# Window attention and a depthwise convolution on one core: where the last taps and the last turn of the fifteenth image stand on VectorE

## The chip, the cores and the metric

The kernel runs on one core of a Trainium2 chip. The time is device time in microseconds (us), from runs of the whole program. PE is the matrix engine, DVE the vector engine, ACT the scalar engine, POOL the GpSimd engine; SP issues DMAs. A trace is one profiled execution.

## The reference

The input x has 16 images of 56 x 56 positions with 384 channels. Two layers follow each other:

```python
x = x + window_attention(group_norm(x))   # 7 x 7 windows, shifted by 3, 12 heads of 32, mask, relative bias
x = x + depthwise_conv(group_norm(x))     # 3 x 3, one filter per channel, weights reduced to their signs
```

Each group norm has 32 groups of 12 channels and takes mean and variance over a whole image. So the second layer of an image can begin only when the first layer of that image is complete.

## The kernel before, in words

Channels lie on the partitions, in three blocks of 128 (c = 0, 1, 2). An image is 8 strips of 7 rows (s counts strips over all images), a strip is 2 units of 4 windows. There are 256 units (u). The loop in `all_units` does, for unit u, the sums of the exponentials (`add_up`, L646, PE), their inverse (`invert`, L685 to L688, ACT and DVE), the products with the values (`attend`, L667), the division (`divide`, L695, DVE), for each second unit the projection (`project`, L706 on PE, L714 and L720 on DVE, a copy L726 on POOL and the store of the strip to a DRAM tile `mid`, L730 and L732), and for unit u + 1 the scores (L576, PE), the softmax's scaling and bias (`softmax`, L593, DVE) and its exponential (`exponential`, L611, ACT).

The second layer of image b - 1 runs beside the first layer of image b. It works in six chunks: half an image (k = 0, 1) of one channel block. For a chunk, `band` loads rows of `mid`, `pad` writes the normalized rows into a padded tile (`hps`, two of them, L798), `middle` writes the centre tap and the residual into a sum (`accs`, two of them, L826 or L828), eight calls of `tap` (L834, DVE) add the other taps into it, `turn_sum` transposes it by blocks of 32 x 32 in place (L841, DVE), and eight calls of `store` (L848, on SP's queue) write it out.

The order of these pieces is written by hand. `at(when, f, ...)` puts a call on a list under a time in units; `all_units` issues the heavy work of unit u in six steps, and after each step the listed calls whose time has come. Each engine executes its instructions in the order of issue. A DMA on SP stands in SP's queue, and what is issued later on SP comes behind it.

The last image (b = 15) has no next image to hide behind. `plan_last` orders its second layer: from unit 254.8 on, `band_late` loads, part 0, the rows that already are in `mid` (L779: into spare tiles, among them `qk` and `bias`), and, part 1, the rows of the last strip. `late_norm` calls `norm_products`, which finds the group means by products with a matrix on PE (L362: `pm` for the means, `pv` for the variances) instead of a trip through DRAM, with short DVE operations in between (L351 to L387). `center` follows (L741 to L745), and then the chunks of channel blocks 0 and 1 with taps on DVE, and channel block 2 as `convolve` on PE (L871, L878), four pieces of 14 rows, whose sums `carry` copies with ACT (L886) and stores. The last two chunks on DVE are turned by PE (L904, L906, L912).

`norm_products` has an argument `meanwhile`: calls to be issued while PE forms the products. The first stands between the products of the means and L375, the rest between the products of the variances and L383. At the start of the program it is used for two weight operations.

The chunk that the change touches is the last one of image 14 (k = 1, c = 2). Its padded tile is the second of `hps`, its sum the second of `accs`. `plan_conv` puts its taps 0 to 8 and its turn at equal distances in units 252 to 254, and its stores, 0.1 units apart, where `plan_last` has the loads of `band_late`, also 0.1 units apart. The sum tile is written again by the second chunk of the last image (L828, o<-qk, on ACT).

Of the kernel before, what the change touches and what calls it, by code (L numbers as in the profile page):

```python
# [22 lines left out]
def group_blocks(nch, gsize, P=128):  # L23

    n = nch // P
    return [
        (k, m)
        for m in range(n)
        for k in range(n)
        if (k * P) // gsize <= ((m + 1) * P - 1) // gsize and (m * P) // gsize <= ((k + 1) * P - 1) // gsize  # L30
    ]
# [3 lines left out]
def kernel(  # L35
# [14 lines left out]
    B, H, W, C = x.shape  # L50
    NH = rel_table.shape[1]
    D = C // NH
    NC = C // P
    HPC = P // D
# [9 lines left out]
    NB = H // BR  # L64
# [28 lines left out]
    def bank(name):  # L93
        return ps.tile([P, 512], F32, tag="mm", name=name)
# [221 lines left out]
    late_tiles = {}  # L316
# [29 lines left out]
    def norm_products(key, gm, meanwhile=()):  # L346
        st = stats.pop(key)
        name = "%d_%d" % key
        mv = small.tile([P, NC, 2], F32, tag="mv", name=f"mv{name}")
        for c in range(NC):  # L350
            nc.vector.bn_aggr(mv[:, c, :], st[:, c].rearrange("p s k -> p (s k)"))  # L351
        if key[0]:
            nc.vector.tensor_tensor(mv[:, :, 0], mv[:, :, 0], bo_sb, ALU.add)

        def group_mean(x, name):
            pg = bank(name)
            pairs = group_blocks(C, GS)
            for m in range(NC):
                of_m = [n for n, (k, j) in enumerate(pairs) if j == m]
                for n in of_m:  # L360
                    k = pairs[n][0]
                    nc.tensor.matmul(  # L362
                        pg[:, 4 * m : 4 * m + 1],
                        gm[:, n, :],
                        x[:, k : k + 1],
                        start=(n == of_m[0]),
                        stop=(n == of_m[-1]),
                    )
            return pg[:, : 4 * NC].rearrange("p (m f) -> p m f", f=4)[:, :, 0]

        mean = group_mean(mv[:, :, 0], f"pm{name}")
        for f, n in meanwhile[:1]:
            f(n)
        dev = small.tile([P, 3, NC], F32, tag="dev_late", name=f"dev{name}", bufs=1)
        nc.vector.tensor_copy(dev[:, 2], mean)  # L375
        nc.vector.tensor_tensor(dev[:, 0], mv[:, :, 0], dev[:, 2], ALU.subtract)
        nc.vector.tensor_tensor(dev[:, 0], dev[:, 0], dev[:, 0], ALU.mult)
        nc.vector.tensor_tensor(dev[:, 0], dev[:, 0], mv[:, :, 1], ALU.add)
        var = seen[:, B : B + NC] if key[0] else dev[:, 0]
        spread = group_mean(dev[:, 0], f"pv{name}")  # L380
        for f, n in meanwhile[1:]:
            f(n)
        nc.vector.tensor_scalar(var, spread, EPS, None, ALU.add)  # L383
        nc.gpsimd.tensor_tensor(dev[:, 1], var, power.to_broadcast([P, NC]), ALU.pow)
        coef = small.tile([P, NC, 2], F32, tag="coef", name=f"coef{name}", bufs=4)
        nc.vector.tensor_copy(coef[:, :, 0], dev[:, 1])
        nc.vector.scalar_tensor_tensor(coef[:, :, 1], dev[:, 2], -1.0, dev[:, 1], ALU.mult, ALU.mult)  # L387
        coefs[key] = coef
# [1 line left out]

    def late_norm(b):
        norm_products((1, b), late_tiles["gm"])

    xs = {}

# [516 lines left out]
    def plan_last(b, first):  # L914

        chunks = [(k, c) for k in range(NB) for c in range(NC - 1)]
        bands_late = [(0, NC - 1), chunks[0], (1, NC - 1), chunks[1], (2, NC - 1), chunks[2], (3, NC - 1)]
        for n, (k, c) in enumerate(bands_late):
            at(first - 1.2 + 0.1 * n, band_late, b, k, c, 0)
            at(first - 0.04 + 0.001 * n, band_late, b, k, c, 1)  # L920
        at(first, late_norm, b)
        at(first + 0.1, center, b, nc.vector)
        for n, (k, c) in enumerate(chunks):
            when = first + 1 + n
            if n == len(chunks) - 1:
                for part in range(2):
                    at(when - 1.9, band_late, b, k, c, part)
            at(when - 0.6 if n else when - 0.13, pad, b, k, c)
            at(when - 0.5 if n else when - 0.12, middle, b, k, c, False, n == 0)
            for i, t in enumerate((0, 1, 2, 3, 5, 6, 7, 8)):  # L930
                at(when + i / 8, tap, b, k, c, t)
            if k == 0:
                at(when + 0.99, turn_sum, b, k, c)
                for part in range(2 * HPC):
                    at(when + 1.01 + 0.05 * part, store, b, k, c, part)
            else:
                for half in range(2):
                    at(when + 1.3 + 0.01 * half, turn_late, b, k, c, half, n == len(chunks) - 1)
            k, c = n, NC - 1
            at(when - 0.3 if n else when - 0.11, pad, b, k, c, True)  # L940
            at(when - 0.25 if n else when - 0.1, middle, b, k, c, True, n == 0)
            at(when + 0.1, convolve, b, k, c, 0)
            at(when + 0.4, convolve, b, k, c, 1)
            at(when + 1.1, carry, b, k, c)
# [4 lines left out]
    def at(when, f, *args):  # L949
        side.setdefault(int(when), []).append((when, f, args))  # L950

    def plan_conv(p, first, step, lead, late, queue):

        at(first, norm_gather, (1, p), queue)
        at(first + 0.1, norm_scale, (1, p), queue)
        at(first + 0.2, center, p)
        first += lead
        for n in range(NB * NC):
            k, c = divmod(n, NC)
            when = first + step * n  # L960
            at(max(when - 1.22 * step, first - lead + 0.5), band, p, k, c)
            at(when - 0.35 * step, pad, p, k, c)
            at(when - 0.25 * step, middle, p, k, c)
            for i, t in enumerate((0, 1, 2, 3, 5, 6, 7, 8)):
                at(when + step * i / 9, tap, p, k, c, t)
            at(when + step * 8 / 9, turn_sum, p, k, c)
            for part in range(2 * HPC):
                at(when + step * 8 / 9 + late + 0.1 * part, store, p, k, c, part)
# [42 lines left out]
    def plan(last_queue):  # L1011
        for b in range(1, B):
            plan_load(b)
            plan_conv(b - 1, NU * b, 2.6 if b < B - 1 else 1.95, 3, 0.4, nc.gpsimd)
        at(B * NU - 6, fetch_late)
        for t in range(9):
            at(B * NU - 5 + 0.3 * t, diagonal, t)
        plan_last(B - 1, B * NU)
# [51 lines left out]
    with tc.manual_schedule():  # L1070
# [7 lines left out]
        gm = bpool.tile([P, BR + 2, R], F32, tag="xb", name="gm_first").rearrange("p h w -> p (h w)")  # L1078
        pairs = len(group_blocks(C, GS))
        gm = gm[:, : pairs * P].rearrange("p (n q) -> p n q", q=P)  # L1080
# [6 lines left out]
        for s in range(NS):  # L1087
            for c in range(NC):
                load(s, c)
        fetch_weights(NC, xpool.tile([P, NC, ST], F32, tag="x", name="wl_out"))  # L1090
        norm_products((0, 0), gm, ((turn_weights, 2), (load_weights, 2)))
        load_bias(nc.sync, 0, 16, True)
        load_bias(nc.gpsimd, T - 1, T, True)
# [94 lines left out]
```

## Time and profile before

| | |
|---|---|
| median of 3 runs | 4023.74 us (4023.71 to 4024.25) |
| the profiled execution | 4024.73 us |
| its span, first to last instruction | 4022.9 us |
| mean granted clock of PE | 0.992 |
| busy: PE, DVE, ACT, POOL | 98%, 87%, 55%, 46% of the span |
| the last softmax (L593) starts | 3911.49 us |
| the last norm's coefficients are there (end of L745) | 3939.17 us |

Starts are in microseconds from the start of the span. In a timeline, a row has start, duration, engine, line, operation and operands; a bracket says how long the engine was idle before and which engine ended that. Rows of the chain of waits have start, duration, engine and line. A row "SPq" is the issue of a DMA by SP; "DMA" is the time until it landed.

### The profile page before, as it was taken

How to read it: one execution, taken by the hardware profiler on the slowest of the kernel's cores; microseconds unless marked ns; L12 is line 12 of the kernel's file. 1: busy time of each engine (PE TensorE's matmuls, PEld its weight loads, DVE VectorE, ACT ScalarE, POOL GpSimd, SP SyncE). 2: the span in 40 equal slices, each digit the busy share in tenths (PEclk: the TensorE clock that was granted, in tenths of full speed). 3: DMA queues.
4: the chain of work that ended last, by engine and by line, in shares of the span. 5: the costliest groups of instructions: out<-in, count | busy, mean ns of one | idle time of the engine just before them, and what ended most of it. 6: DMA issues, size and time to landing. Idle time of an engine off the chain costs nothing.

```text
span 4022.9 us, 144682 instructions
## 1 busy us (share of the span) xinstructions
PE 3948.1 (98%) x63189; PEld 2412.3 (60%) x63189; DVE 3495.0 (87%) x3719; ACT 2229.5 (55%) x4690; POOL 1865.7 (46%) x3151
## 2 busy tenths in 40 slices
PE   8999999999999999999999999999999999999987
PEld 5565655555556555555656556565655656556657
DVE  5547989899898988989899898988989899898897
ACT  4545556565565655556565565655555555565542
POOL 5544645355454554545355554554545355452000
PEclk9999999999999999999999999999999999999998
DMA  4324445455444545455455444544455454543444
GB/s 116 81 67 106 105 112 114 109 119 116 105 113 101 129 110 112 107 116 115 111 118 114 109 111 102 129 109 112 103 117 115 106 122 114 110 113 82 111 113 95
DMA packets 801076, 439.36 MB, mean 109 GB/s; under 512 B 671274, under 2 KB 750489, under 8 KB 800432
## 3 DMA queue, kind: packets, MB, share of 16 engines
q1 hardware_dynamic: 711334, 268.44, 30.7%
q0 software_dynamic: 87808, 161.15, 17.0%
q8 instruction: 498, 8.16, 0.9%
q14 instruction: 146, 1.20, 0.1%
q10 hardware_dynamic: 1290, 0.42, 0.0%
HBM read 170.08 MB, written 158.45 MB: 82 GB/s over the span
## 4 chain that ended last, share of the span: by engine, by line
PE 48%; DVE 16%; issue 14%; POOL 11%; DMA 7%; ACT 2%; SPq 1%; DVEq 0%; POOLq 0%; ACTq 0%
PE pq L509 19%; PE py L706 10%; PE pv L522 10%; POOL xl L456 7%; DVE o L834 7%; PE score_banks L576 4%; PE po L667 3%; PE score_banks L646 2%; DVE e L593 2%; DVE xt L473 2%; DMA xl<-in_x_dram 1%; DMA mvd<-mv 1%; DMA mid<-y 1%; DVE st L489 1%; DVE ln L688 1%
## 5 line engine op out<-in xcount | busy, mean ns | idle before, releaser
L509 PE MATMUL pq<-xn,wq_t 128*128 128x392 f32 x4608 | 1584.9, 496 | 0.0
L456 POOL DMA_DIRECT2D xl<-in_x_dram x1980 | 1332.6, 725 | 144.7 <-DVE xt L473 94.9
L834 DVE SCALAR_TENSOR_TENSOR o<-hp,dw_t,o 128x1568 f32<-128x1568 f32 x752 | 1378.2, 1833 | 5.4
L509 PEld LDWEIGHTS pq<-xn,wq_t 128*128 128x128 f32 x4608 | 845.4, 188 | 595.6 <-ACT ln L685 0.4
L522 PE MATMUL pv<-xn,wq_t 128*128 128x392 f32 x2304 | 813.4, 496 | 13.7 <-DVE y L714 13.7
L706 PE MATMUL py<-ot,wo_t 128*128 128x392 f32 x2304 | 817.9, 500 | 7.8 <-DVE ot L695 6.8
L516 ACT COPY qk<-pq 128x392 f32<-128x392 f32 x768 | 368.4, 483 | 561.8 <-PE pq L509 561.2
L726 POOL COPY y<-y 128x63 f32<-128x63 f32 x128 | 61.4, 480 | 1221.0 <-DVE y L714 1220.9
L706 PEld LDWEIGHTS py<-ot,wo_t 128*128 128x128 f32 x2304 | 425.1, 190 | 311.5 <-DVE ot L695 25.8
L522 PEld LDWEIGHTS pv<-xn,wq_t 128*128 128x128 f32 x2304 | 423.1, 188 | 312.0 <-DVE y L714 15.7
L611 ACT ACTIVATE e<-e 128x1176 f32<-128x1176 f32 x256 | 303.2, 1185 | 493.3 <-DVE e L593 492.2
L687 DVE SCALAR_TENSOR_TENSOR ln<-score_banks,inv 128x588 f32<-128x588 f32 x256 | 195.8, 765 | 322.3 <-ACT inv L686 321.6
L529 ACT COPY vt<-pv 128x392 f32<-128x392 f32 x384 | 189.1, 492 | 367.1 <-PE pv L522 366.3
L576 PEld LDWEIGHTS score_banks<-qk 32*49 32x49 f32 x24576 | 265.8, 118 | 145.3 <-issue 114.6
L593 DVE SCALAR_TENSOR_TENSOR e<-score_banks,bias 128x1176 f32<-128x1176 f32 x256 | 347.0, 1355 | 5.9 <-PE score_banks L576 5.9
L667 PEld LDWEIGHTS po<-e,v 49*32 49x32 f32 x24576 | 310.4, 105 | 52.2 <-issue 2.8
L485 ACT COPY x<-xt 128x196 f32<-128x196 f32 x720 | 225.5, 367 | 172.8 <-DVE xt L473 172.6
L667 PE MATMUL po<-e,v 49*32 49x49 f32 x24576 | 308.8, 212 | 2.1 <-issue 2.0
L576 PE MATMUL score_banks<-qk 32*49 32x49 f32 x24576 | 298.0, 218 | 3.1 <-DVE ln L687 3.1
L533 DVE STREAM_TRANSPOSE vq<-vt 128x512 f32<-128x512 f32 x384 | 265.4, 693 | 7.2 <-ACT vt L529 4.1
L498 ACT ACTIVATE xn<-x,coef 128x392 f32<-128x392 f32 x384 | 247.1, 711 | 4.5 <-DVE coef L387 4.5
L714 DVE TENSOR_TENSOR y<-py,x 128x392 f32<-128x392 f32 x384 | 213.1, 555 | 41.7 <-PE py L706 41.1
(183 smaller groups left out, 3296.2 us busy)
## 6 DMA issues: line engine op xcount, KB each, us to landing
v<-vq SPq DMA_DIRECT2D x2048, 48.0 KB
xb<-mid SPq DMA_DIRECT2D x90, 855.5 KB
out_dram<-o SPq DMA_DIRECT2D x736, 98.0 KB
mid<-y POOLq DMA_DIRECT2D x112, 619.5 KB
xl<-in_x_dram POOLq DMA_DIRECT2D x1260, 52.5 KB
mid<-y POOLq DMA_DIRECT2D x15, 354.0 KB
xl<-in_x_dram POOLq DMA_DIRECT2D x180, 28.0 KB
mid<-y POOLq DMA_DIRECT2D x15, 265.5 KB
```

Of the source, the lines that this page charges most:

```text
L456: nc.gpsimd.dma_start(xz[i * D + lo : i * D + hi, c, k : k + n, :], flat[token : token + n * (hi - lo)].rearrange("(k t) c -> t k c", k=n) ...
L498: nc.scalar.activation(xn[:, c, :, :T], xs[s][:, c, :].rearrange("p (w t) -> p w t", t=T), AF.Identity, bias=coef[:, c, 1:2], scale=coef[: ...
L509: nc.tensor.matmul(pq[:, :ST].rearrange("p (w t) -> p w t", t=T), wq_t[:, c, m * P : (m + 1) * P], xn[:, c, :, :T], start=(c == 0), stop=( ...
L516: nc.scalar.copy(qk[:, m, :ST], pq[:, :ST])
L522: nc.tensor.matmul(pv[:, :ST].rearrange("p (w t) -> p w t", t=T), wq_t[:, c, 2 * C + m * P : 2 * C + (m + 1) * P], xn[:, c, :, :T], start= ...
L533: nc.vector.transpose(vq[:, :, :, m].rearrange("p h n d -> p n h d"), vt[:, m].rearrange("p (n w) (j b) -> p n (w j) b", w=2, b=D),)
L576: nc.tensor.matmul(pp[row * HT : row * HT + rows, i, k0 : k0 + T], qk[part, NC * fast + j, q0 : q0 + rows], qk[part, NC * (not fast) + j, ...
L593: nc.vector.scalar_tensor_tensor(e, pp[:, :, : NC * 2 * T].rearrange("q i (n k) -> q i n k", k=T), QSCALE, bias[:, int(s % NS == NS - 1)]. ...
L611: nc.scalar.activation(flat, flat, AF.Exp, accum_out=reach[:, 0, u : u + 1])
L667: nc.tensor.matmul(po[w][i * D : (i + 1) * D, (2 * j + r) * T : (2 * j + r + 1) * T], vs[s][keys, i, n * 2 + r, j], by_head(u)[keys, i * N ...
L706: nc.tensor.matmul(py[:, :ST], wo_t[:, c, m * P : (m + 1) * P], ots[s][:, c, :], start=(c == 0), stop=(c == NC - 1),)
L834: nc.vector.scalar_tensor_tensor(acc, by_half(hp[:, dy : dy + BR, dx : dx + W]), dw_t[:, c, t : t + 1], acc, ALU.mult, ALU.add)
```

## The change

The last chunk of image 14 keeps taps 0, 1, 2, 3, 5 and 6 where they were. Tap 7 is issued at 254.4 (256 - 1.6), which is behind the softmax of unit 255; tap 8 at 255.1, behind the division of unit 255; and the turn is handed to `late_norm` as its `meanwhile`, so that it stands between L353 and L375. The eight stores are issued behind the norm, at 256.02 and on, which puts them on SP behind the store of the last strip and all loads of `band_late`, and ahead of the stores of the last image. The two loops over `meanwhile` take any number of arguments. On DVE the order around the last softmax becomes: L695 (unit 254), L593, tap 7, L687, L688, L695 (unit 255), tap 8, L714. No instruction is added or removed.

```diff
-        for f, n in meanwhile[:1]:
-            f(n)
+        for f, *args in meanwhile[:1]:
+            f(*args)
...
-        for f, n in meanwhile[1:]:
-            f(n)
+        for f, *args in meanwhile[1:]:
+            f(*args)
...
-    def late_norm(b):
-        norm_products((1, b), late_tiles["gm"])
+    def late_norm(b, behind):
+        norm_products((1, b), late_tiles["gm"], (behind,))
...
-        at(first, late_norm, b)
+        k, c = NB - 1, NC - 1
+        for t, ahead in ((7, 1.6), (8, 0.9)):
+            at(first - ahead, tap, b - 1, k, c, t)
+        at(first, late_norm, b, (turn_sum, b - 1, k, c))
+        for part in range(2 * HPC):
+            at(first + 0.02 + 0.001 * part, store, b - 1, k, c, part)
...
-            for i, t in enumerate((0, 1, 2, 3, 5, 6, 7, 8)):
+            close = p == B - 2 and n == NB * NC - 1
+            for i, t in enumerate((0, 1, 2, 3, 5, 6, 7, 8)[: 6 if close else 8]):
                 at(when + step * i / 9, tap, p, k, c, t)
+            if close:
+                continue
             at(when + step * 8 / 9, turn_sum, p, k, c)
```

## Prediction

> **What bounds the kernel now.** The busy table has PE at 98% of the span and DVE at 87%, but these are means over sixteen images, and the change touches only the last 120 us. So I read the chain of waits first, for that stretch, and then the timeline of the engines that it names. From 3907 us on the chain goes through DVE, not PE:
>
> ```profile
> 3906.30 1.46 PE L576 MATMUL score_banks<-qk 32*49 32x49 f32 x96 [3.10 <-DVE ln L687]
> 3907.16 0.77 DVE L695 TENSOR_TENSOR ot<-ot,ln 128x588 f32<-128x588 f32 x1
> 3907.85 3.73 DVE L834 SCALAR_TENSOR_TENSOR o<-hp,dw_t,o 128x1568 f32<-128x1568 f32 x2
> 3911.49 1.38 DVE L593 SCALAR_TENSOR_TENSOR e<-score_banks,bias 128x1176 f32<-128x1176 f32 x1
> 3912.79 2.03 DVE L841 STREAM_TRANSPOSE o<-o 128x1792 f32<-128x1792 f32 x1
> 3917.17 0.77 DVE L687 SCALAR_TENSOR_TENSOR ln<-score_banks,inv 128x588 f32<-128x588 f32 x1 [2.35 <-ACT inv L686]
> 3918.85 0.77 DVE L695 TENSOR_TENSOR ot<-ot,ln 128x588 f32<-128x588 f32 x1
> 3923.81 0.57 DVE L714 TENSOR_TENSOR y<-py,x 128x392 f32<-128x392 f32 x1 [4.19 <-PE py L706]
> ...
> 3929.70 0.16 DVE L353 TENSOR_TENSOR mv<-mv,bo_sb 128x3 f32<-128x3 f32 x1
> 3932.91 0.16 DVE L375 COPY dev<-pm 128x3 f32<-128x3 f32 x1 [3.05 <-PE pm L362]
> ```
>
> The columns are start, duration, engine, line; the bracket is idle time and who ended it. The last scores are complete at 3906.30 + 1.46 = 3907.76, and the last softmax (L593) starts only at 3911.49: for 3.7 us PE and ACT have nothing, because DVE does taps 7 and 8 of image 14 first. After that DVE waits three times, 2.35, 4.19 and 3.05 us, each for a result that goes back to this softmax. In the first gap the turn (2.03 us) is already hidden.
>
> The chain view shows what runs beside the norm, on SP's queue:
>
> ```profile
> 3926.85 0.41 SPq L848
> 3927.31 3.41 SPq L848
> 3930.82 0.70 SPq L730
> 3931.57 4.30 DMA mid<-y
> 3935.88 0.36 SPq L779
> ...
> 3937.28 2.03 DMA bias<-mid
> 3939.35 1.87 DVE o L826
> ```
>
> The last strip's rows (L730, L732) go to DRAM and come back (L779); the first operation of the last convolution, L826, starts when both this and the norm are through. Its idle time is put down to the DMA, but it is 0.17 us: the last norm row on DVE (L745) ends at 3939.17. Two paths, equal within 0.2 us. Behind L826 the work runs in one line to the end: taps, turn, stores, then ACT and PE.
>
> ```profile
> 3973.10 1.70 ACT L828 ACTIVATE o<-bias,cen 128x1568 f32<-128x1568 f32 x1 [12.52 <-DMA out_dram<-o]
> 3974.70 1.13 ACT L798 ACTIVATE xl<-xb_late,coef 128x896 f32<-128x896 f32 x1
> 3975.88 3.76 PE L871 MATMUL pc<-xl,xl 128*114 128x128 f32 x16 [3.73 <-ACT xl L798]
> ```
>
> From 3975.88 PE has no gap that the chain leaves until 4009. So a shift of L826 reaches the end in full.
>
> **The change, part by part.**
>
> *Taps 7 and 8 leave the place before L593.* DVE is free behind L695 at 3907.16 + 0.77 = 3907.93, the scores are there at 3907.76, so L593 starts at about 3907.95: 3911.49 - 3907.95 = **3.54 us earlier**. The pair cost 3.73, the rest is the distance from the scores. Everything that hangs on L593 (exponential, sums, inverse, division, projection, norm) follows.
>
> *Tap 7 behind L593.* 1.86 us (half of 3.73), where L687 waits for the inverse. From the end of L593 (3912.87) to L687 (3917.17) there are 4.30 us; the turn that lay there goes. Cost 0, with 2.4 us over.
>
> *Tap 8 behind the division.* 1.86 us in the 4.19 us in which DVE waits for the projection. Nothing of PE waits on the tap; cost 0, 2.3 us over.
>
> *The turn in the norm.* 2.03 us behind L353, in the 3.05 us until the group means (pm) are back. Cost 0, with 1.0 us over: the thinnest cover. If pm came in half its 2.87 us (a PE at full clock; it ran at half nearly throughout), 0.4 us of the turn would stick out, less than pm itself saved.
>
> *The eight stores of this chunk.* Before, they alternate with the band loads on SP, and all wait for the turn: the second load starts at 3915.33, behind a store that waited until 3914.8. Afterwards the seven loads follow each other from 3904.7, held only by what they read and overwrite; the last such condition is the bias tile, free with L593 at 3909.3. The DMA engines were idle from 3909 to 3913 and about fully busy from 3917 to 3930, so the loads gain 6 us or more. L730 needs the copy on POOL (ends 3928.64, then 3925.10); before, it stood 2.18 us behind it on SP, 3.41 us of which is one store. With no store ahead it starts near 3925.2, and by the row above L826's data is there 3939.31 - 3930.82 = 8.5 us later, 3933.7. The norm ends at 3939.17 - 3.54 = 3935.63. So the norm alone sets L826, and 0.13 of the 0.17 us idle goes too.
>
> *What waits for the stores now.* They stand behind the five last loads, from about 3932.5, and the turn is done by then (3926.2 + 2.05 = 3928.3). Behind them on SP are only the stores of the next chunk (ready at 3955). ACT's L828 o<-qk overwrites the tile that they read; it would run at 3943.08 - 3.6 = 3939.5. The trace has two such groups: 3958.5 (turn done) to 3973.1 with loads and other stores between, 14.6 us, and 3975.5 to 3987.16, 11.7 us. That gives 3944 to 3947, so ACT waits 5 to 8 us, with L798 hp_late and L828 acc_late behind it. These end by 3951, and PE needs them at 3958.24 - 3.6 = 3954.6, DVE its sum at 3954.8. Cost 0, with 3.6 us over at worst.
>
> *The clock of PE.* Rows of half a microsecond in which the granted clock changes (the last three columns are this clock, the DMA share and GB/s):
>
> ```profile
> 3923.00:3923.50 0.50, 0.50 (x2) 0.34 (x1) 0.00 (x0) 0.00 (x0) 0.00 (x0) 0.55 0.78 256
> 3930.00:3930.50 0.50, 0.49 (x4) 0.50 (x4) 0.00 (x0) 0.00 (x0) 0.00 (x0) 0.78 0.95 183
> 3947.00:3947.50 0.50, 0.50 (x5) 0.50 (x4) 0.48 (x1) 0.00 (x0) 0.00 (x0) 0.66 0.00 0
> 3974.50:3975.00 0.50, 0.00 (x0) 0.00 (x0) 0.50 (x1) 0.50 (x2) 0.00 (x0) 0.65 0.00 0
> 3981.00:3981.50 0.50, 0.50 (x4) 0.50 (x4) 0.46 (x2) 0.00 (x0) 0.00 (x0) 0.52 0.98 148
> ```
>
> 0.55 over half a microsecond is 0.05 us at 1.0 behind 0.45 at 0.5, so the change is at 3923.45; likewise 3930.28, 3947.34, 3974.65, 3981.48. The distances are 6.83, 17.06, 27.31 and 6.83: 2, 5, 8 and 2 times 3.41. The clock changes on a grid that doesn't move with the work. Two slow stretches are on the path: the projection (3919.68 to 3923.45, 3.77 us) and the third late convolution (3975.88 to 3981.48, 5.60 us). Work that comes 3.54 us sooner meets the grid one step of 3.41 sooner: 0.13 us more at half clock in each, 0.07 us lost twice. [...]
>
> **Sum:** -3.54 - 0.13 + 0.14 = -3.5 us. The profiled execution took 4024.73 us (span 4022.9 and 1.8 around it) and becomes 4021.2. The median of the three runs is 4023.74, 1.0 below; the same step gives **4020.2 us**, 0.09% less.
>
> **The rivals.**
>
> *The clock grid falls otherwise.* Its phase against the program may differ between executions. The trace's slow stretches behind a pause last 3.77, 5.71 (3941.63 to 3947.34) and 5.60 us: 1.9 us apart, 0.97 us of work. If the projection gets the long one, the gain is 2.6 us, 4021.2; if the third convolution gets the short one, 4.5 us, 4019.3. For it: the profiled execution is 1.0 us above the median, about one such difference. Against: the three runs lie within 0.54 us.
>
> *SP remains where it was* and the change doesn't do what it says. If the seven loads hold the queue as long as before, L730 stays at 3930.8 and L826 at 3939.3, with nothing gained: 4023.7. For it: the two paths were level, and the DMA engines were about full from 3917 on. Against: the loads start 6 us sooner, and only 2 us of slack would have to be eaten before any of the gain goes.
>
> *The late stores hold ACT,* and it gets slower. Landing at time L, they free hp_late and acc_late at L + 1.7 + 1.1 + 1.0. PE idled 3.73 us before the third convolution, so PE may start the second up to that much behind 3958.24 without loss to the old time: L = 3958.2 is the point, 25.7 us behind the first issue at 3932.5. The rows give 11.7 and 14.6. At twice the longer, 29.2 us, L is 3961.7 and the kernel 3.5 us slower than before: 4027.2. For it: the eight stores now lie in one block of 128-byte pieces. Against: almost nothing else is on the DMA engines then (share 0.00 to 0.01 from 3941 to 3957).
>
> **How the numbers follow.** Forecast 0.72; the grid otherwise 0.13; SP 0.08; late stores 0.05; something else that I don't see 0.02. The range takes in the forecast and both ends of the grid, with half a microsecond for the spread of runs: 4018.8 to 4021.8; SP and the stores are left out. 0.2% is 8 us, about what a measurement of this kernel can tell from no change; every case lies within it except a store block that lands still later. Same 0.95, faster 0.02, slower 0.03.
>
> **What the changed profile would show.** L593 directly behind L695, 0.1 to 0.2 us after the scores. L834 between L593 and L687, and again between L695 and L714, with L687 still released by ACT and L714 by PE. L841 between L353 and L375, with about 1 us idle left before L375. L730 within 0.3 us of the POOL copy, and L826 with no DMA as releaser, near 3935.7. ACT's L828 o<-qk released by out_dram<-o between 3939 and 3947. PE's third late convolution near 3972.4. I am wrong if L375 or L714 waits for nothing but DVE, if L826 is still released by bias<-mid later than 3936, or if PE stops between its first and second late convolution.

## The result, and the profile after

The changed kernel takes **4018.09 us** (median of 19 runs, 4015.50 to 4021.35) against 4024.25 for the kernel before (19 runs, 4020.94 to 4029.55): ratio 0.9984, 95% interval 0.9978 to 0.9991. That is 6.2 us less where 3.5 was forecast, and 4018.09 lies below the range of 4018.8 to 4021.8. The profiled execution took 4016.54 us (4024.73 before), with a span of 4014.7 (4022.9).

DVE around the last softmax, in the timeline of the changed kernel:

```profile
3905.92 0.77 DVE L695 TENSOR_TENSOR ot<-ot,ln 128x588 f32<-128x588 f32 x1
3906.61 1.38 DVE L593 SCALAR_TENSOR_TENSOR e<-score_banks,bias 128x1176 f32<-128x1176 f32 x1
3907.90 1.84 DVE L834 SCALAR_TENSOR_TENSOR o<-hp,dw_t,o 128x1568 f32<-128x1568 f32 x1
3912.28 0.77 DVE L687 SCALAR_TENSOR_TENSOR ln<-score_banks,inv 128x588 f32<-128x588 f32 x1 [2.54 <-ACT inv L686]
...
3914.65 1.84 DVE L834 SCALAR_TENSOR_TENSOR o<-hp,dw_t,o 128x1568 f32<-128x1568 f32 x1
3919.11 0.57 DVE L714 TENSOR_TENSOR y<-py,x 128x392 f32<-128x392 f32 x1 [2.62 <-PE py L706]
...
3925.73 2.04 DVE L841 STREAM_TRANSPOSE o<-o 128x1792 f32<-128x1792 f32 x1
3928.08 0.16 DVE L375 COPY dev<-pm 128x3 f32<-128x3 f32 x1 [0.32 <-PE pm L362]
...
3934.19 0.15 DVE L745 TENSOR_TENSOR cen<-cen,bo_sb 128x3 f32<-128x3 f32 x1
3934.52 1.86 DVE L826 TENSOR_SCALAR o<-xb,cen 128x1568 f32<-128x1568 f32 x1 [0.17 <-DMA out_dram<-o]
```

L593 now starts 0.69 us behind the start of L695 (4.33 before). Both taps and the turn lie in the three waits, and each wait still ends with ACT or PE, not with DVE's own work. The turn's cover is the thinnest, as foreseen: 0.32 us are left.

SP and ACT in the same profile:

```profile
3924.62 0.62 SPq L730 DMA_DIRECT2D mid<-y  x1
3925.29 0.62 SPq L732 DMA_DIRECT2D mid<-y  x1
3928.61 0.33 SPq L779 DMA_DIRECT2D xb_late<-mid  x1
...
3930.40 0.43 SPq L779 DMA_DIRECT2D xb_late<-mid  x1
3930.93 23.64 SPq L848 DMA_DIRECT2D out_dram<-o  x10
```

```profile
3938.67 1.71 ACT L828 ACTIVATE o<-qk,cen 128x1568 f32<-128x1568 f32 x1 [0.33 <-DVE o L834]
```

L730 follows the copy on POOL (3924.35 to 3924.60) at once, and the last loads are issued by 3930.83, 3.7 us ahead of L826 (3934.52). The eight stores stand behind them (the row of ten also holds two of the next chunk), and ACT waits 0.33 us for its tile.

To see where 8.2 us of span went, I cut both profiles at the same instructions, by the starts in the timelines:

| stretch | before | after | difference |
|---|---|---|---|
| start to L695 of unit 254 | 3907.16 | 3905.92 | -1.24 |
| to L593 of unit 255 | 4.33 | 0.69 | **-3.64** |
| to L353 (projection in it) | 18.21 | 19.04 | +0.83 |
| to L375 (first group products) | 3.21 | 2.43 | -0.78 |
| to L826 | 6.44 | 6.44 | 0 |
| to the third late convolution | 36.53 | 36.04 | -0.49 |
| to the last product of the last L904 | 33.49 | 32.44 | **-1.05** |
| to the end of the last DVE instruction (L1123; L1131 in the changed kernel) | 3.16 | 3.21 | +0.05 |
| to the end of the span | 10.41 | 8.54 | **-1.87** |

The first row can't come from the change, since DVE and PE execute the same work up to there; among the profiles below of kernels that do so it scatters from 3904.4 to 3907.6. From L695 to L826 the change gave 32.19 - 28.60 = 3.59 us, nearly what was forecast. The last row was not in the forecast at all. SP's own waits at the end of the span show what it is, before and after:

```profile
SPq L1126 <- SPq L1126: 5.1, 2, 2.6
```

```profile
SPq L1134 <- SPq L1134: 2.8, 1, 2.8
```

The columns are total, number and longest. L1126 (L1134 with the longer file) is the branch behind which the second pass is skipped. Before, SP is held twice behind it, and after once. In the trace of before, SP executes the first of a row of semaphore waits 2.63 us behind the branch, the second 2.47 us later, and the rest 0.1 us apart; in the changed kernel the first comes at 2.82 and the second 0.10 later.

This made a theory. No call is added by the change, but "No instruction is added or removed", as the section on the change has it, is not true of the waits in the built program: the trace of the changed kernel has 3343 instructions on SP against 3342, one wait more, and two waits more each on ACT and DVE. The second pass has one more wait on SP too; I counted that one in the built program, and no trace shows it, since the pass is not executed. The code behind the branch lies behind both passes, so it lies two instructions further on. **Theory A:** the two holds are fetches of code, and whether the second is needed hangs on the place of the code behind the branch; the change has moved it to a place where one is enough. **Theory B:** all 6 us come from the order on DVE and SP. A third reading, that SP's second wait is for a store, falls by the trace of before: the last store on that wait's semaphore had landed at 4015.81, and the wait is executed at 4020.76.

### The profile page after: what moved, and what is told of

Read it like the earlier page. It is cut to its first block, busy times and chain, and to the rows that moved or that the text cites. A ratio compares the mean times of both kernels' runs of the same rounds, so it can differ in the third digit from the quotient of the medians.

```text
span 4014.7 us, 144687 instructions
## 1 busy us (share of the span) xinstructions
PE 3946.9 (98%) x63189; PEld 2410.3 (60%) x63189; DVE 3495.4 (87%) x3719; ACT 2227.6 (55%) x4690; POOL 1860.8 (46%) x3151
## 3 DMA queue, kind: packets, MB, share of 16 engines
q8 instruction: 498, 8.16, 0.9%
## 4 chain that ended last, share of the span: by engine, by line
PE 39%; issue 19%; DVE 16%; POOL 15%; DMA 6%; ACT 2%; SPq 1%; DVEq 0%; POOLq 0%; ACTq 0%
PE pq L509 15%; POOL xl L456 11%; PE pv L522 8%; PE py L706 8%; DVE o L834 7%; PE score_banks L576 3%; PE po L667 2%; DVE e L593 2%; PE score_banks L646 2%; DVE xt L473 2%; DMA xl<-in_x_dram 1%; DMA mvd<-mv 1%; DVE ln L688 1%; DVE st L489 1%; DVE vq L533 1%
## 5 line engine op out<-in xcount | busy, mean ns | idle before, releaser
L687 DVE SCALAR_TENSOR_TENSOR ln<-score_banks,inv 128x588 f32<-128x588 f32 x256 | 196.0, 765 | 320.9 <-ACT inv L686 320.0
L593 DVE SCALAR_TENSOR_TENSOR e<-score_banks,bias 128x1176 f32<-128x1176 f32 x256 | 347.1, 1356 | 5.9 <-PE score_banks L576 5.9
L714 DVE TENSOR_TENSOR y<-py,x 128x392 f32<-128x392 f32 x384 | 213.4, 556 | 41.0 <-PE py L706 37.5
```

The source lines that it names most:

```text
L593: nc.vector.scalar_tensor_tensor(e, pp[:, :, : NC * 2 * T].rearrange("q i (n k) -> q i n k", k=T), QSCALE, bias[:, int(s % NS == NS - 1)]. ...
```

## The experiments

Each kernel was timed 11 times, beside 33 runs of the kernel before on the same chip: their median is 4023.47 us for the two kernels with added SP instructions, the first try with the stores and the single full-clock kernel, and 4023.69 for the rest.

### One more SP instruction that is never executed

```diff
             clear_again()
+            for _ in range(1):
+                nc.sync.dma_start(worst[:, 0:1], b_out[0:P].unsqueeze(1))
             load_bias(nc.gpsimd, 0, T, False)
```

This is the kernel before, with a DMA (and one wait) added to the second pass.

> The kernel before, with one more SP DMA in the second pass, the branch that is not taken. What is executed is the same as before, but SP's code behind the branch lies two instructions further on. Theory A (place of the code): in the profile of before, SP executes the first of eight waits behind its branch at 4018.29 us and the second only at 4020.76, and in the profile of the change all eight stand together at 4012.51 to 4013.05; the gap is a code fetch that the change lost only because it adds two SP instructions. Then this kernel has no such gap, the stretch from the last DVE instruction (L1123) to the end of the span falls from 10.4 to about 8.5 us, and the median is 1.5 to 2.3 us below the kernel before. Theory B (the whole gain comes from the order on DVE and SP): nothing changes, within 0.5 us of before, and the gap stays.

4021.36 us (4019.72 to 4025.09), 2.1 us below before by the medians; the ratio, 0.9994 with an interval of 0.9985 to 1.0003, doesn't exclude 1 by itself, though nine of the eleven runs lie below the lowest of the 33 beside them (4022.03). The profile is plain: the end stretch is 7.89 us (10.41), and the double wait is gone:

```profile
SPq L1126 <- SPq L1126: 2.6, 1, 2.6
```

L695 to L826 took 32.25 us, as before. So about 2 us hang on the place of the code, which here only an instruction that never runs has moved.

### The changed kernel with the code moved back

The same loop with `range(247)` in the changed kernel: 254 instructions with their waits, 256 with the two of the change. The question is whether the second hold is back at this distance from the place in the kernel before; that 256 is the distance to try was a guess that no run had shown.

> [...] Theory A: the gap of about 2.4 us between SP's first and second wait behind the branch comes back, the end stretch is about 10.4 us instead of 8.5, and the gain over before shrinks from 6 to about 4 us. Theory B: it stays at about 6 us.

4020.37 us (4018.22 to 4023.18; ratio 0.9994, 0.9985 to 1.0003), 3.1 below before by the medians. L695 to L826 took 28.74 us, so the order is that of the change, and the double wait is back:

```profile
SPq L1134 <- SPq L1134: 5.6, 2, 3.5
```

The end stretch is 12.14 us, longer than expected, because SP came to the branch late (4.37 us behind the last DVE instruction, 3.13 before) and the first wait came late too (3.51 us behind the branch). By the profile theory A holds and theory B falls; the interval of the times alone, from a gain of 6 us to a loss of 1, doesn't decide between them. Below, "the old place" stands for this place too, 256 instructions behind that of the kernel before. With the code in its old place the order is worth 3.1 us by the medians, and the profile's 32.19 - 28.74 = 3.45 us is the firmer number.

### Stores among the loads, first try

The changed kernel with the turn behind tap 8 and the stores at their old times.

> The changed kernel, but the turn stands right behind tap 8 (behind the division) and the eight stores are back among the first loads of the last image's bands on SP. Taps as in the change. Theory of the prediction, SP's part: the second load now waits for a turn that ends about 12.6 us behind the start of the division of unit 254 instead of 7.7, so L730 comes about 16 us after that and L826 8.5 us after L730: about 37 us from the start of that division to L826 (32.2 before, 28.6 with the change), released by the DMA; the time is about 5 us above before and 11 above the change. Rival (the norm alone sets L826, where the stores stand is of no account): 28.6 us, and the time of the change.

4019.05 us (ratio 0.9989, 0.9979 to 0.9998), and 30.80 us from L695 to L826: neither. At their old times three of the stores were issued ahead of the moved turn and did not wait for it: this kernel stores the chunk in part unturned. It can't test what was expected, which was about stores that wait. Nor are the 2.2 us more than in the change mainly a matter of SP's queue. The norm ends 1.9 us later behind L695 than in the change: tap 8 stood idle for 3.87 us, which the profile puts down to out_dram<-o (the early stores read the sum that it writes), and the group means came back later (3.47 us from L353 to L375, 2.43 in the change). Only the last 0.3 us are a wait for the loads.

### Stores among the loads, behind the turn

```diff
+        at(first - 0.899, turn_sum, b - 1, k, c)
+        for part in range(2 * HPC):
+            at(first - 0.895 + 0.01 * part, store, b - 1, k, c, part)
...
-            at(first - 1.2 + 0.1 * n, band_late, b, k, c, 0)
+            at(first - 1.2 if n == 0 else first - 0.9 + 0.01 * n, band_late, b, k, c, 0)
```

> The changed kernel with the turn right behind tap 8 and the eight stores between the loads in SP's queue, as before the change, this time issued behind the turn, so that the first of them waits for it (in the run before this one they were issued ahead of it). SP's code behind the branch has the place of the kernel before. Theory of the prediction: SP sets L826, about 37 us behind the start of L695 of unit 254 (32.2 before), by the DMA; about 5 us slower than before. Rival (the norm alone): 28.6 us, 3.5 us faster than before.

4026.14 us (4023.65 to 4027.93; ratio 1.0005, interval 0.9996 to 1.0015): 2.5 us above before and 8.4 above the change. L826 came 35.10 us behind L695, 32.19 before and 28.60 in the change; so 6.5 of the 8.4 us come from this order, and the code behind the branch has its old place here, which in the change it has not. DVE's timeline shows who was late:

```profile
3935.48 0.15 DVE L745 TENSOR_TENSOR cen<-cen,bo_sb 128x3 f32<-128x3 f32 x1
3942.31 1.49 DVE L826 TENSOR_SCALAR o<-xb,cen 128x1568 f32<-128x1568 f32 x1 [6.67 <-DMA xb<-mid]
```

The norm is ready and the loads are not. The forecast's reading of SP was right in kind; the size, 37 us, was 2 too high. The first store waited until 3919.89, 12.7 us behind L695 (12.6 expected), but L730 came 14.8 us after that (16 expected) and L826 7.7 us after L730 (8.5 expected).

### Stores alone behind the norm

The kernel before, with the eight stores moved as in the change and nothing else.

> The kernel before, with only the eight stores moved behind the norm; taps 7 and 8 and the turn stay ahead of and behind the last softmax. SP's code behind the branch has the place of the kernel before. Theory of the prediction (the norm and SP were level, so that SP alone gives at most 0.2 us): 32.1 us from L695 to L826, the time of before within 0.5 us. Rival (the way through SP held more than the profile shows): 1 us or more below before.

4023.10 us (4022.24 to 4025.93; ratio 1.0, 0.9991 to 1.0009), and 32.27 us from L695 to L826. With the softmax late, nothing is gained by a free SP queue. The double wait is there (5.6, 2, 3.0 in its row), as in every kernel whose code has the old place. So the stores must leave the loads' place for the later turn to pay, and moved alone they pay nothing.

### The changed kernel again

> The changed kernel once more, beside the others of this call. Theory A (3.5 us from the order, about 2.2 us from the place of SP's code): 5 to 6.5 us below before; in the profile 28.6 to 28.8 us from the division of unit 254 (L695) to L826, against 32.2 before, and an end stretch from L1131 to the end of the span near 8.5 us, against 10.4. Theory B (all of the 6 us is the order): the stretch from L695 to L826 and what follows it has to carry more than 4 us.

4017.72 us (4015.93 to 4021.90), 6.0 below before (ratio 0.9987, 0.9978 to 0.9996). L695 to L826 took 28.60 us, the end stretch 7.98.

### PE kept at full clock ahead of the third convolution

```diff
+    def keep_warm(count):
+        for i in range(count):
+            nc.tensor.transpose(score_banks[:, 0, :P], ident, ident)
...
+            if n == 2:
+                at(when - 0.31, keep_warm, 30)
             at(when - 0.3 if n else when - 0.11, pad, b, k, c, True)
```

> The changed kernel with 30 more products of 128 columns on PE, into score banks that nobody reads any more, between the second and the third late convolution, where PE idles for 4.1 us and its clock is halved for the start of the third (3.4 us of half clock in the profile of the change, 5.6 in that of before). About 3.6 us at full clock, so that they end before ACT lets the third convolution begin. Theory (the clock behind this pause is on the path): full clock from the start, 1.7 to 2.8 us less than the change, so 4015.3 to 4016.4 beside its 4018.1. Rival (PE isn't the bound there, or the products delay it): no gain, or up to 1 us slower.

4016.29 us (4014.20 to 4020.26; ratio 0.9983, 0.9974 to 0.9992), 7.2 below before. PE's timeline:

```profile
3964.39 3.44 PE L917 MATMUL score_banks<-ident 128*128 128x128 f32 x30
3969.47 2.00 PE L871 MATMUL pc<-xl,xl 128*114 128x128 f32 x16 [1.64 <-ACT xl L798]
...
3999.42 1.72 PE L904 MATMUL px<-ident,o 128*128 128x128 f32 x14 [0.44 <-DVE o L834]
```

The granted clock is 1.00 in each row of 2 us from 3964 to 3974. The first sixteen products take 2.00 us instead of 2.92, and the stretch to the last L904 falls from 32.44 to 31.40, by 1.04 us where 1.7 to 2.8 were expected. It would have fallen further, but now DVE's last tap ends a wait of 0.44 us ahead of L904: the next bound is 1 us away. The median lies within the expected 4015.3 to 4016.4 only because the kernel before was 0.8 us faster beside it than beside the change; against before, the gain grew from 6.2 to 7.2 us.

### Products that nobody reads in five pauses of PE

The same helper with banks of its own, 20 products behind `attend` of units 254 and 255 and behind the last scores, 14 ahead of the group means, and the 30.

> The changed kernel with products that nobody reads in five pauses of PE: 20 behind the products with the values of units 254 and 255, 20 behind the last scores, 14 ahead of the group means, 30 ahead of the third late convolution. Theory (the halved clock is on the path at the projection, the norm's products and the third convolution): full clock from 3900 us to the norm's end and in the third convolution, the projection's 18 products in about 6.3 us instead of 8 to 9, the norm's two in 1.7 each; 4 to 6 us below the change. Rival (products that wait or that stand in the way): scores or projection begin later, and the gain is under 2 us or a loss.

4015.31 us (4013.22 to 4016.80; ratio 0.9979, 0.9970 to 0.9988): the fastest here, 8.4 below before and 2.4 below the change, less than expected. The profiled execution, 4016.80, is the slowest of its eleven. The projection took 6.09 us (8.89 in the change), but PE paused for 2.05 us among the products with the values, with nothing that the profile shows as its cause, and the 20 products behind it took 0.20 us each, where the 30 of the experiment before took 0.11 each, at a clock of 1.00:

```profile
3915.35 0.68 PE L669 MATMUL po<-e,v 49*32 49x49 f32 x49 [2.05 <-issue]
3915.96 4.07 PE L920 MATMUL warm<-ident 128*128 128x128 f32 x20
3919.86 6.09 PE L708 MATMUL py<-ot,wo_t 128*128 128x392 f32 x18
```

Whether that pause belongs to this program or to this execution was not tried. The second of the norm's products still took 3.12 us, where 1.7 was expected, and L375 follows the turn with no idle time: with the means back sooner, the turn is the next bound there.

### All profiles side by side

| kernel | L695 to L826 | third convolution to last L904 | end stretch | SP: second wait behind the first |
|---|---|---|---|---|
| before | 32.19 | 33.49 | 10.41 | 2.47 |
| stores alone | 32.27 | 32.44 | 10.76 | 2.99 |
| stores among the loads | 35.10 | 32.44 | 10.78 | 2.99 |
| change, code moved back | 28.74 | 33.34 | 12.14 | 2.09 |
| stores among the loads, first try | 30.80 | 32.43 | 8.53 | 0.10 |
| before, one SP instruction more | 32.25 | 32.44 | 7.89 | 0.11 |
| change | 28.60 | 32.44 | 8.54 | 0.10 |
| change again | 28.60 | 32.44 | 7.98 | 0.10 |
| change, full clock once | 28.70 | 31.40 | 8.16 | 0.10 |
| change, products in five pauses | 27.77 | 31.17 | 7.60 | 0.10 |

The two effects stand apart. The first column goes with the order, the last two with the place of SP's code: a mean end stretch of 11.0 us for the upper four, 8.1 for the lower six. It is SP's code that matters: the kernel with the stores alone has the two waits more on ACT and on DVE and SP's old count of 3342, and is held twice; the first try with the stores has SP's 3343 and the old counts on ACT and DVE, and is held once.

The traces hold a sign of the fetch. The DMA queue that carries instructions moved, from shortly before the last DVE instruction to the end of the span, before and after (packets, MB, share):

```profile
q14 instruction: 9, 0.07, 2.3%
```

```profile
q14 instruction: 8, 0.07, 2.5%
```

In all ten traces such a packet starts 0.56 to 0.83 us behind SP's first wait. In the upper four, and only there, another starts 0.63 to 0.88 us behind the second: that is the one packet more. The queue moved seven other packets in each of the two windows above, and the trace doesn't say for which engine; that these packets are SP's is read from their steady distance. So in these four each of SP's two holds has a packet of its own.

## Why the prediction was wrong, and where it was right

*Right: the taps.* L593 was to come 3.54 us sooner against L695; it came 3.64 sooner. Tap 7, tap 8 and the turn cost nothing, with 2.5, 2.6 and 0.3 us left; the forecast said 2.4, 2.3 and 1.0. The last is smaller because the group products ran partly at full clock (2.09 us for 2.87; they began at 3925.96, and the clock fell to 0.50 at 3927.10), the case that the forecast named.

*Right: SP's part.* L730 follows the copy, and the norm alone sets L826. Both controls bear it out: the stores alone move nothing, and the stores among the loads take the gain away and 2.9 us more from L695 to L826. One reading beside it was loose: L730 can't have 3.41 us of one store in its 2.18 us behind the copy; that store was issued from 3927.31, 1.33 us ahead of the copy's end.

*Right in its answer, wrong in its size: the late stores.* ACT was to wait 5 to 8 us for them and waited 0.33. The profile puts that down to DVE, but in the trace ACT's wait for the semaphore of the eighth store ends at 3938.47, directly behind that store's landing at 3938.44. So the stores did hold ACT, at no cost: PE's second late convolution still follows the first without a gap. The two rows that I took gave 14.6 and 11.7 us for such a group; here the last landed 7.5 us behind the first issue, 8.2 us in the second profile of the change (ACT waited 1.30) and 9.1 us in the one with products in five pauses (2.51). Both of those rows had other stores between, the first loads too; whether that made them slower was not tried.

*Wrong, and small: the idle time of L826.* The 0.17 us that the profile puts down to a DMA is no wait for data. It is 0.17 us after the change too, where the loads had landed by 3932.6, and the kernel with products in five pauses has 0.18, put down to the last norm row on DVE itself. In the traces DVE's queue steps through four wait instructions ahead of L826, 0.10 us apart, and L826 starts 0.05 us behind the last of them. The term of -0.13 is 0.

*Wrong, and no part of the change: the clock.* The sum had +0.07 for each of two stretches, on the assumption that the grid keeps its place against the program. It does not: its step is 3.41 us as forecast, but its phase differs between the two profiles: counted from L695 of unit 254, the clock is back at 1.00 after 16.29 us before and after 14.35 in the change, 1.94 apart. In the changed kernel's profile (last columns again clock, DMA share, GB/s) they are at

```profile
3920.00:3920.50 0.50, 0.50 (x2) 0.24 (x1) 0.28 (x1) 0.00 (x0) 0.00 (x0) 0.73 0.00 0
3971.00:3971.50 0.50, 0.50 (x7) 0.50 (x6) 0.50 (x1) 0.50 (x2) 0.00 (x0) 0.97 0.00 0
3974.50:3975.00 0.50, 0.50 (x5) 0.50 (x4) 0.50 (x1) 0.00 (x0) 0.00 (x0) 0.61 0.77 182
```

By the same reading as in the prediction that is 3920.27, 3971.47 and 3974.89, 51.20 and 3.42 us apart, 15 steps and one: the projection has 5.49 us at half clock (3.77 before) and the third convolution 3.41 (5.60 before). It is the rival "the grid falls otherwise", with both of its halves at once: +0.83, -0.78 for the group products, -1.05. The sum over the pair of profiles is -1.0, but it is no gain of the change: the kernel before with one dead instruction has the same 32.44 us. That the 3.59 us from L695 to L826 come so near to the forecast is partly luck: the clock took 0.83 us there at the projection and gave 0.78 at the group products. The -0.49 ahead of the third convolution lies within what that stretch shows elsewhere, 35.88 to 36.66 us.

*Wrong: the end.* "A shift of L826 reaches the end in full" was true; that nothing else changes behind it was assumed and not looked at. The sum, -3.54 - 0.13 + 0.14, has no term for the stretch behind the last DVE instruction, and so puts it at nothing without a reason. This is **the step that failed**, and it is the term that was missing: about 2 us by the pads' medians (4023.47 to 4021.36 in the kernel before; with the change, 3.1 us of gain with the code moved back and 6.0 to 6.2 with it where the change puts it, so 3). The trace of before showed it, as two waits of SP behind the branch. The runs show two holds (2.6 to 3.6 us to the first wait in all of them, 2.1 to 3.0 more where the code has the old place) and the packets above, of 8 KB each in the profiles of before and after; that the holds are fetches of code is inferred from these packets. The second hold is gone with the code two instructions further on and back with it 256 further on. Why it hangs on the place is not shown; no trace lists addresses.

The sum in measured terms: 3.6 us for the order and some 2 to 3 us for the place of the code make 5.6 to 6.6, against 6.2 by the 19 runs and 6.0 by the 11.

What stays open: why the work up to L695 takes 3904.4 to 3907.6 us in programs that do the same there, which places of the code bring the second hold, and what held PE in the last experiment.

## What to carry to other kernels

A step that stands between a finished result and the operation that many engines wait for can be moved behind it for nearly its full time (here 3.64 us of 3.73), if each piece fits into a wait that another engine ends; then look at the queue that the moved piece's transfers block, because here 6.5 us hung on it. Follow the chain to the end of the span, not to the last instruction that computes, and count the built instructions per engine when code lies behind a branch: two instructions that are never executed moved about 2 us in the kernel before. A difference of this size between two programs is only explained when the same code place, and the same clock stretches, have been compared.

## What the runs showed of the hardware

- The place of the code behind the taken branch cost time here: with the code in its old place SP was held a second time for 2.1 to 3.0 us, with one more packet of instructions (four profiles); otherwise it went on after 0.10 or 0.11 us (six profiles).
- PE's clock changed between 1.00 and 0.50 at multiples of 3.41 us, in the profiles of before and of the change; counted from L695, the same change of it came 1.94 us apart in the two. The slow stretch of the third convolution was 5.60 us long before, 3.41 in the change and 0 with the products ahead of it (clock 1.00), with 33.49, 32.44 and 31.40 us for the same work.
- Products that nobody reads, in a pause of 4.1 us, were worth 1.04 us in the profile, and then DVE was the next to be late.
